# One product's two matmuls put into two different places of TensorE's order in a Mamba-2 mixer kernel

## The chip, the core and the metric

The kernel runs on one core of a Trainium2 chip. The metric is the device time of one execution in microseconds; shorter is better. In what follows PE is TensorE, the matrix engine (PEld its weight loads), DVE is VectorE, ACT is ScalarE, POOL is GpSimd and SP the engine that issues most DMAs. A line such as L846 is line 846 of the kernel.

## What is computed

A layer norm of x (4 sequences of 256 tokens, 512 channels) feeds two branches, a Mamba-2 state-space mixer and a gated feed-forward network. Their outputs are multiplied and added to x. Cut to what matters here, the mixer is:

```python
zxbcdt = hidden_states @ in_proj_w.T            # 512 -> 8192 gate, 8192 x, 1024 B, 1024 C, 128 dt
gate, xBC, dt = split(zxbcdt)
xBC = silu(causal_conv(xBC, conv_w, 4 taps) + conv_b)
x, B, C = split(xBC)                            # 128 heads of 64 channels, 8 groups
dt = softplus(dt + dt_bias)
# chunked scan: y = (C B^T * decay) (x * dt) + carried states
y = (Y_diag + Y_off) + D * x
y = y * silu(gate)
y = group_rms_norm(y) * norm_w
s = y @ out_proj_w.T
out = x_in + s * silu(ffn(layernorm(x_in)))
```

## The kernel before

A first stage (front, up to about 310 us of the span) makes the layer norm, the feed-forward branch, dt, and for each of the 8 groups the scores of B and C. Everything here concerns the second stage, a loop `for i in range(CT + 2)` over 64 channel tiles of 128 channels (two heads each). Iteration i works on three tiles at once: it projects tile i (`here`), computes the scan of tile i - 1 (`old`) and gates tile i - 2 (`older`). From iteration 10 on it also does a part of the output projection of an earlier group (`project_out`, with `og` the group and `on` the place 0 to 7 in it). The order on every engine is the order in which the code is written out by hand; each engine works off its own queue in that order and waits by semaphores for the others.

The projection of tile i takes seven products instead of eight, in Strassen's manner in the variant with fewer sums: a 2 x 2 arrangement of half the tokens by half of the 512 input channels, for gate and x together. A product is two logical matmuls of 128 x 128 weights by 512 tokens (k = 0 and 1); the profile shows each as two instructions, so a product is x4 there. They share three PSUM banks, px, pq and pz. In the order in which PE runs them, with the names that the text uses:

- P1: `product(px, a11, x11, True)`, L821. ACT then copies px to pz (L822), so that pz can go on by itself.
- P5: `product(pq, s1, t1, True)`, L830.
- P6: `product(px, s2, t2, False)`, L831, on top of P1 in px. ACT copies px out to gT (L832).
- P2: `product(pz, a12, x21, False)`, L837, on top of the copy in pz. Its sum is read much later, by the SiLU at L895.
- P7: `product(px, s3, t3, False)`, L845, again on px, after L832 has read it. ACT copies px out to xpad (L846).
- P4: `product(px, a22, t4, False)`, L876, once more on px, after L846 has read it. ACT copies it out at L877.
- P3: `product(pq, s4, x22, False)`, L881, on pq, after DVE has added the earlier sum in pq to xpad (L869, which itself follows L846). DVE adds P3's result to gT at L885.

All the products' matmuls stand under L173, the line in the helper `product`. In the profile's groups P1 is px<-xnT,w, P5 is pq<-xc,s, P6 is px<-xc,s, P2 is pz<-xnT,w, P7 and P4 are both px<-xc,w, and P3 is pq<-xnT,s.

Between them lies the work on tile i - 1. ACT finishes its convolution with a SiLU (`conv_silu`, L186: at the end of the iteration before for tiles from 9 on, at L825 of this one for tiles 0 to 8, as `LEAD` is 9) and makes exponentials of the decay (L615). DVE multiplies decays by scores (`meet`, L618 and L619). ACT starts the output banks (`y_begin`, L651). PE transposes block 0 of the tile, four transposes into the bank tp (T0, L624, called by `values_0`), and DVE scales it twice into v (L632). After P3, `values_1` does the same with block 1 (T1, and L641) in the same bank, of which there is one. In the end `y_products` (L665) multiplies v by the decays; DVE's convolution taps (L181), the sums of the next weights (L142 to L146) and a scan (L612) close the iteration. L672 (`y_gate`) opens the next one on DVE.

When `on` is 0 (iterations 10, 18, 26 and so on to 58) PE also runs `norm_sums` (L683, 16 small instructions) directly behind P7. When `on` is even, DVE makes `left_sums` (L701 to L704) ahead of L869.

So before the change PE's order around the place is P6, P2, P7, (norm_sums), T0, P4, P3, T1.

Of the kernel before, what the change touches and what calls it, by code (L numbers as in the profile page):

```python
# [57 lines left out]
KT = HID // P  # L58
# [23 lines left out]
def mixer_ffn(ctx: ExitStack, tc: tile.TileContext, x, in_w, conv_w, conv_b, dt_bias, a_log, d_col,  # L82
# [66 lines left out]
    def factors(w, s):  # L149
        a11, a12, a21, a22 = blocks(w)  # L150
        return a11, a12, a22, s[:, 0], s[:, 1], s[:, 2], a21

    def combine_w(w):
        s = scp.tile([P, 3, KT // 2, P], F32, name="s")
        for _ in combine_to(s[:, 0], s[:, 1], s[:, 2], blocks(w)[2], w):
            pass
        return factors(w, s)

    x11, x12, x21, x22 = [xnT[:, k:k + 2, h:h + HALF] for k in (0, 2) for h in (0, HALF)]
# [7 lines left out]
    def by_batch(v):  # L167
        return v.rearrange("p (b l) -> p b l", l=L)

    def product(pp, a, b, start):  # L170

        for k in range(KT // 2):
            nc.tensor.matmul(pp, a[:, k, :], b[:, k, :], start=start and k == 0,  # L173
                             stop=k == KT // 2 - 1, skip_group_check=not start)

# [13 lines left out]
    def front(pre, one_of, fp, f2, hp, wq):  # L189
# [223 lines left out]
        def bc_pieces(g):  # L413
# [7 lines left out]
            for a, b, to in ((a11, x11, cpad_h[0]), (s2, t2, cpad_h[1]), (s3, t3, bpad_h[1]),  # L421
                             (a22, t4, bpad_h[0])):
                product(px, a, b, a is a11)
                nc.scalar.copy(to, by_batch(px))
                if a is s2:
                    s = scp.tile([P, 3, KT // 2, P], F32, name="s")
                    held["a"] = factors(w, s)
                    sums = combine_to(s[:, 0], s[:, 1], s[:, 2], blocks(w)[2], w)
                if a is not a11:
                    next(sums, None)  # L430
                yield
            pz = ps_proj.tile([P, HALF], F32, name="pz", tag="proj")
            product(pz, a12, x21, True)
            nc.vector.tensor_add(cpad_h[0], cpad_h[0], by_batch(pz))
            pq = ps_proj.tile([P, HALF], F32, name="pq", tag="proj")
            product(pq, s1, t1, True)
            nc.vector.tensor_add(bpad_h[1], bpad_h[1], by_batch(pq))
            yield
# [136 lines left out]
    with (tc.manual_schedule(), tc.tile_pool(name="pre", bufs=NT) as pre,  # L575
# [3 lines left out]
        a = front(pre, one_of, fp, f2, hp, wq)  # L579
# [31 lines left out]
    def decay_scan(m):  # L611
        nc.vector.tensor_tensor_scan(m, m, after, 0.0, ALU.add, ALU.mult)  # L612

    def decay_exp(m):
        nc.scalar.activation(m, m, AF.Exp)  # L615

    def meet(m, off):
        nc.vector.tensor_mul(m, m, gm[:, 0:T])  # L618
        nc.vector.tensor_mul(off, off, gm[:, T:])  # L619

    def transposed(xT, c):
        tp = ps_t.tile([P, NB, P], F32, name="tp", tag="t")
        for b in range(NB):
            nc.tensor.transpose(tp[:, b, :], xT[:, b, c * P:(c + 1) * P], ident)  # L624
        return tp

    def values_0(ct, xT):

        tp, vs = transposed(xT, 0), []
        for f in (dt[:, 0], dt_tail):  # L630
            v = xsp.tile([P, NB, 2, HD], F32, name="v")
            nc.vector.tensor_tensor(  # L632
                v, tp.rearrange("p b (h d) -> p b h d", d=HD),
                f[:, :, 2 * ct:2 * ct + 2].unsqueeze(3).to_broadcast([P, NB, 2, HD]), ALU.mult)
            vs.append(v)
        return vs
# [9 lines left out]
    def y_begin(ct, xT):  # L646

        ps = []
        for i in range(2):
            py = ps_y.tile([P, 2, L], F32, name="py", tag="y")  # L650
            nc.scalar.mul(py, xT[:, 2 * i:2 * i + 2, :], dcol[:, ct:ct + 1])  # L651
            ps.append(py)
        return ps
# [107 lines left out]
    with tc.manual_schedule():  # L761
        nc.sync.dma_start(gm, scores[0])
        ms, offs = {0: load_rows(0)}, {0: load_off(0)}
        xTs, gTs, yps, wos, rights, toms = {}, {}, {}, {}, {}, {}
        sqacc = rs = ya = outs = left = nxt = ob = sa = sb = sc = None
        for i in range(CT + 2):
# [49 lines left out]
            if here:  # L816
                a11, a12, a22, s1, s2, s4, s3 = a
                px, pq, pz = [ps_proj.tile([P, HALF], F32, name=f"p{n}", tag="proj")
                              for n in "xqz"]
# [9 lines left out]
            if here:  # L829
                product(pq, s1, t1, True)  # L830
                product(px, s2, t2, False)  # L831
                nc.scalar.copy(gT[:, HALF:], px)  # L832
                if lead:
                    decay_exp(ms[i - 1][1])
                if i:
                    decay_scan(ms[i][0])
                product(pz, a12, x21, False)  # L837
            if old:
                meet(ms[i - 1][0], offs[i - 1][0])
                meet(ms[i - 1][1], offs[i - 1][1])  # L840
                if r == 0 and here:
                    nc.sync.dma_start(gm, scores[g])
                yps[i - 1] = y_begin(i - 1, xTs[i - 1])
            if here:
                product(px, s3, t3, False)  # L845
                nc.scalar.copy(xpad_h[1], by_batch(px))  # L846
            if og >= 0 and on == 0:
                sd = norm_sums(sqacc)
# [19 lines left out]
            if here:  # L868
                nc.vector.tensor_add(xpad_h[1], xpad_h[1], by_batch(pq))  # L869
            if old:  # L870
                vs = values_0(i - 1, xTs[i - 1])
            for n, turn in ((wg, PER_G - 1), (og, 0), (og, 1)):
                if i < CT + 1 and n >= 0 and on == turn:
                    toms[n].pop(0)()
# [32 lines left out]
            if here:  # L907
# [4 lines left out]
                if i + 1 <= EARLY:  # L912
                    s = scp.tile([P, 3, KT // 2, P], F32, name="s")
                    nc.sync.dma_start(s, early[i, :, 0:3])
                    a = factors(w, s)
                elif i + 1 < CT:
                    a = combine_w(w)
# [20 lines left out]
            if wg >= 0 and wg < G:  # L938
                if wn == 0:
                    wos[wg] = wop.tile([P, PER_G, HID], F32, name="wo")  # L940
                for k in range(PER_G):
                    if wn == come(k):
                        ct = wg * PER_G + k
# [14 lines left out]
        for b in range(NB):  # L958
            a, f, xb = whole[b]
# [75 lines left out]
```

## Time and profile before

| what | value |
|---|---|
| median of 3 runs | 1793.18 us (1792.14 to 1793.36) |
| the profiled execution, its own time | 1795.49 us |
| its span, from the first instruction to the last | 1793.0 us |
| PE busy | 1742.7 us (97%) |
| DVE busy | 1448.6 us (81%) |
| ACT busy | 1066.0 us (59%) |
| mean granted PE clock | 0.994 of full speed |

A profile is one execution. Its page gives the busy time of each engine, the chain of work that ended last, and groups of equal instructions with the idle time of the engine just ahead of them and what ended it. Matmuls are pipelined: one of 512 columns is shown with about 0.59 us although the next starts 0.43 us later, so a busy PE isn't PE at its peak, and an idle time is counted only from the modelled end of the last matmul.

### The profile page before, as it was taken

How to read it: one execution, taken by the hardware profiler on the slowest of the kernel's cores; microseconds unless marked ns; L12 is line 12 of the kernel's file. 1: busy time of each engine (PE TensorE's matmuls, PEld its weight loads, DVE VectorE, ACT ScalarE, POOL GpSimd, SP SyncE). 2: the span in 40 equal slices, each digit the busy share in tenths (PEclk: the TensorE clock that was granted, in tenths of full speed). 3: DMA queues.
4: the chain of work that ended last, by engine and by line, in shares of the span. 5: the costliest groups of instructions: out<-in, count | busy, mean ns of one | idle time of the engine just before them, and what ended most of it. 6: DMA issues, size and time to landing. Idle time of an engine off the chain costs nothing.

```text
span 1793.0 us, 22592 instructions
## 1 busy us (share of the span) xinstructions
PE 1742.7 (97%) x8494; PEld 1117.4 (62%) x8494; DVE 1448.6 (81%) x1740; ACT 1066.0 (59%) x1417; POOL 197.3 (11%) x239
## 2 busy tenths in 40 slices
PE   9999999999899999999999999999999999999989
PEld 6566666455466666666666666666666666666667
DVE  5758675799988888888888888888888888888846
ACT  4544343577666666666666666666666666666630
POOL 3221221000000000111011101110111011101110
PEclk9999999999999999999999999999999999999989
DMA  6254643566846665767676767676777676766674
GB/s 223 80 185 155 212 162 123 196 223 215 253 138 203 195 210 178 201 197 210 180 202 197 210 182 203 197 208 185 203 197 209 185 203 197 208 185 203 179 211 141
DMA packets 164235, 342.69 MB, mean 191 GB/s; under 512 B 15392, under 2 KB 55968, under 8 KB 164128
## 3 DMA queue, kind: packets, MB, share of 16 engines
q1 hardware_dynamic: 141296, 287.78, 46.3%
q0 software_dynamic: 22832, 53.49, 16.8%
q8 instruction: 67, 1.10, 0.2%
q14 instruction: 40, 0.33, 0.1%
HBM read 236.08 MB, written 76.28 MB: 174 GB/s over the span
## 4 chain that ended last, share of the span: by engine, by line
PE 89%; DVE 6%; ACT 4%; issue 1%; DMA 1%; ACTq 0%; DVEq 0%; SPq 0%
PE px L173 27%; PE po L721 21%; PE pq L173 13%; PE py L665 9%; PE pz L173 7%; PE pp L285 4%; PE pf L293 2%; ACT xpad L846 2%; PE tp L624 2%; PE pg L460 1%; DVE cT L181 1%; PE pv L683 1%; DVE xT L181 1%; DVE bT L181 1%; DVE m L612 0%
## 5 line engine op out<-in xcount | busy, mean ns | idle before, releaser
L173 PE MATMUL px<-xc,w 128*128 128x512 f32 x576 | 278.7, 606 | 19.4 <-ACT xpad L846 14.1
L612 DVE TENSOR_TENSOR_SCAN m<-m,after 128x1024 f32<-128x1024 f32 x128 | 292.0, 2282 | 0.0
L181 DVE SCALAR_TENSOR_TENSOR xT<-xpad,cw,xT 128x1024 f32<-128x1024 f32 x192 | 246.2, 1282 | 4.6
L173 PEld LDWEIGHTS px<-xc,w 128*128 128x128 f32 x576 | 104.2, 190 | 136.3 <-issue 97.4
L721 PE MATMUL po<-wo,ya 128*128 128x256 f32 x768 | 178.4, 382 | 0.0
L665 PE MATMUL py<-m,v 128*64 128x128 f32 x2048 | 162.2, 278 | 3.9 <-DVE v L641 3.9
L618 DVE TENSOR_TENSOR m<-m,gm 128x1024 f32<-128x1024 f32 x128 | 154.8, 1209 | 8.9 <-ACT m L615 8.9
L721 PEld LDWEIGHTS po<-wo,ya 128*128 128x128 f32 x768 | 142.6, 192 | 17.6 <-issue 0.3
L904 POOL DMA_DIRECT2D sqacc<-sq x55 | 46.9, 853 | 931.1 <-ACT sq L860 927.3
L173 PE MATMUL px<-xc,s 128*128 128x512 f32 x288 | 137.5, 600 | 5.0 <-ACT pz L822 2.2
L173 PE MATMUL px<-xnT,w 128*128 128x512 f32 x288 | 141.9, 615 | 0.0
L173 PE MATMUL pq<-xnT,s 128*128 128x512 f32 x288 | 136.2, 595 | 1.1 <-DVE xpad L869 1.1
L615 ACT ACTIVATE m<-m 128x1024 f32<-128x1024 f32 x128 | 135.4, 1058 | 0.7
L173 PE MATMUL pq<-xc,s 128*128 128x512 f32 x288 | 135.4, 592 | 0.3 <-DVE gT L885 0.3
L173 PE MATMUL pz<-xnT,w 128*128 128x512 f32 x288 | 135.3, 592 | 0.0
L665 PEld LDWEIGHTS py<-m,v 128*64 128x64 f32 x2048 | 118.0, 138 | 26.2 <-issue 19.7
L721 PE MATMUL po<-tw,sy 128*128 128x256 f32 x512 | 117.1, 382 | 1.2 <-ACT sa L775 1.2
L869 DVE TENSOR_TENSOR xpad<-xpad,pq 128x512 f32<-128x512 f32 x64 | 43.7, 683 | 80.3 <-ACT xpad L846 80.3
L721 PEld LDWEIGHTS po<-tw,sy 128*128 128x128 f32 x512 | 98.1, 192 | 15.2 <-ACT sa L775 1.6
L624 PEld LDWEIGHTS tp<-ident,xT 128*128 128x128 f32 x512 | 64.3, 143 | 67.8 <-issue 67.2
L672 DVE TENSOR_TENSOR yg<-py,gT 128x512 f32<-128x512 f32 x128 | 83.8, 678 | 22.7 <-PE py L665 22.7
L173 PEld LDWEIGHTS px<-xc,s 128*128 128x128 f32 x288 | 54.7, 192 | 73.0 <-issue 65.8
(172 smaller groups left out, 3059.8 us busy)
## 6 DMA issues: line engine op xcount, KB each, us to landing
m<-rows SPq DMA_DIRECT2D x128, 512.0 KB, 6.4
w<-in_in_w SPq DMA_DIRECT2D x133, 256.0 KB, 6.8
mo<-rows SPq DMA_DIRECT2D x128, 256.0 KB, 7.2
gated<-yg SPq DMA_DIRECT2D x64, 512.0 KB, 8.2
ya<-gated SPq DMA_DIRECT2D x30, 1024.0 KB, 7.1
sqacc<-sq POOLq DMA_DIRECT2D x55, 512.0 KB, 5.4
wo<-in_out_w SPq DMA_DIRECT2D x64, 256.0 KB, 7.1
acc<-sa POOLq DMA_DIRECT2D x24, 512.0 KB, 5.9
```

What stands on the lines that cost most here:

```text
L173: nc.tensor.matmul(pp, a[:, k, :], b[:, k, :], start=start and k == 0, stop=k == KT // 2 - 1, skip_group_check=not start)
L181: nc.vector.scalar_tensor_tensor(xT, xpad[:, :, k:k + L], cw[:, i, k:k + 1], xT, ALU.mult, ALU.add)
L285: nc.tensor.matmul(pp, w[:, k * P:(k + 1) * P], part[:, k, :], start=(k == 0 and part is xh), stop=(k == KT - 1 and part is xl))
L612: nc.vector.tensor_tensor_scan(m, m, after, 0.0, ALU.add, ALU.mult)
L615: nc.scalar.activation(m, m, AF.Exp)
L618: nc.vector.tensor_mul(m, m, gm[:, 0:T])
L624: nc.tensor.transpose(tp[:, b, :], xT[:, b, c * P:(c + 1) * P], ident)
L665: nc.tensor.matmul(py[d, q * P:(q + 1) * P], v[:, b, h, :], m, start=False, stop=stop, skip_group_check=True)
L672: nc.vector.tensor_mul(yg[:, 2 * i:2 * i + 2, :], ps[i], by_batch(gT[:, i * HALF:(i + 1) * HALF]))
L721: nc.tensor.matmul(po, a[:, k, :], b[:, k, :], start=start and k == 0, stop=k == HG - 1, skip_group_check=not start)
L869: nc.vector.tensor_add(xpad_h[1], xpad_h[1], by_batch(pq))
L904: nc.gpsimd.dma_start(sqacc, sq, accum_op=ALU.add)
```

## The change

P2's two matmuls are separated. The one for k = 0 stays where P2 was, between P6 and P7. The four transposes T0 are moved from `values_0` to directly behind it, still ahead of P7. The one for k = 1 moves behind P7 (and ahead of norm_sums, where there is one), so ahead of P4. `values_0` is handed the bank tp instead of filling it; DVE's two multiplications in it stay at their place. PE's order becomes P6, P2 (k = 0), T0, P7, P2 (k = 1), (norm_sums), P4, P3, T1. The other engines' orders and all DMAs are as before. In iteration 0 there is no T0, and in iteration 64 there are no products.

```diff
-    def product(pp, a, b, start):
+    def product(pp, a, b, start, ks=range(KT // 2)):
 
-        for k in range(KT // 2):
+        for k in ks:
             nc.tensor.matmul(pp, a[:, k, :], b[:, k, :], start=start and k == 0,
                              stop=k == KT // 2 - 1, skip_group_check=not start)
...
-    def values_0(ct, xT):
+    def values_0(ct, tp):
 
-        tp, vs = transposed(xT, 0), []
+        vs = []
         for f in (dt[:, 0], dt_tail):
...
-                product(pz, a12, x21, False)
+
+                product(pz, a12, x21, False, (0,))
             if old:
+                tp0 = transposed(xTs[i - 1], 0)
                 meet(ms[i - 1][0], offs[i - 1][0])
                 meet(ms[i - 1][1], offs[i - 1][1])
...
             if here:
                 product(px, s3, t3, False)
+                product(pz, a12, x21, False, (1,))
                 nc.scalar.copy(xpad_h[1], by_batch(px))
...
             if old:
-                vs = values_0(i - 1, xTs[i - 1])
+                vs = values_0(i - 1, tp0)
```

## The prediction

> **What bounds the kernel now.** I read the page first: shares of the engines, the chain that ended last, then the groups of instructions for the idle time ahead of TensorE.
>
> ```profile
> PE 1742.7 (97%) x8494; PEld 1117.4 (62%) x8494; DVE 1448.6 (81%) x1740; ACT 1066.0 (59%) x1417; POOL 197.3 (11%) x239
> PE 89%; DVE 6%; ACT 4%; issue 1%; DMA 1%; ACTq 0%; DVEq 0%; SPq 0%
> L173 PE MATMUL px<-xc,w 128*128 128x512 f32 x576 | 278.7, 606 | 19.4 <-ACT xpad L846 14.1
> ```
>
> TensorE (PE) is busy 97% of the span and makes 89% of the chain, so time is won only where PE stands still. The last line says where: ahead of the products px<-xc,w (P7 and P4), most of it ended by ACT's copy at L846. The view of waits, for PE alone, counts them:
>
> ```profile
> PE px L173 <- ACT xpad L846: 14.1, 57, 0.7
> PE px L173 <- ACT gT L832: 2.4, 1, 2.4
> ```
>
> Fifty-seven of the 64 iterations have that wait. P4 accumulates on the bank px that L846 has just read, so it waits for the copy. The chain of waits shows one such place (iteration 41) and the next iteration, which has none:
>
> ```profile
> 1192.85 1.72 PE px L173 x4
> 1194.56 1.72 PE pz L173 x4
> 1196.28 1.73 PE px L173 x4
> 1198.01 0.02 issue
> 1198.03 0.59 ACT xpad L846
> 1198.63 0.04 issue
> 1198.67 1.98 PE px L173 x4
> 1200.65 1.72 PE pq L173 x4
> ...
> 1217.83 1.72 PE px L173 x4
> 1219.54 1.68 PE pv L683 x16
> 1221.22 0.49 PE tp L624 x4
> 1221.71 1.72 PE px L173 x4
> ```
>
> The rows are P6, P2, P7, the wait, P4, P3; then P7, norm_sums, transposes, P4. In a stream a product takes 1.72 (four instructions, 0.43 apart) and four transposes 0.44. After the wait P4 takes 1.98: it also fills the pipeline, and its first weight load is no longer hidden. The wait therefore costs more than the idle column's 0.24: from P7's end to P4's end 0.65 + 1.98 = 2.63 us, where transposes and P4 in a stream need 0.44 + 1.72 = 2.16. So 0.47 us a time. Where norm_sums (1.68) stands in the hole, nothing is lost.
>
> The timeline of iteration 41 shows both copies and the gated weight load:
>
> ```profile
> 1194.60 0.59 ACT L832 COPY gT<-px 128x512 f32<-128x512 f32 x1 [1.89 <-PE px L173]
> 1198.03 0.59 ACT L846 COPY xpad<-px 128x512 f32<-128x512 f32 x1 [1.65 <-PE px L173]
> 1198.67 0.30 PEld L173 LDWEIGHTS px<-xc,w 128*128 128x128 f32 x2 [0.48 <-ACT xpad L846]
> ```
>
> Both copies find ACT idle (1.89 and 1.65 us), so each begins the moment PE ends. Each needs a cover of about 0.65 us on PE. Behind P6 the cover is P2, 1.72 us: 1.07 too much. Behind P7 it is the transposes, 0.44: 0.21 too little.
>
> **The change part by part.** It adds no instruction. It moves, on PE's queue alone, two matmuls of P2 (with two weight loads) past P7, and four transposes T0 ahead of P7 (past norm_sums too, where it stands). ACT, DVE, SP and POOL keep their order; no DMA moves.
>
> Part 1, T0 earlier. T0 needs xT of the iteration before and the bank tp free; behind it would wait P7 and all of PE. xT: the SiLU (L186) ended at 1208.40 + 1.14 = 1209.54 for an iteration whose P7 started at 1217.66. In iterations 1 to 9 the SiLU is younger (399.47 + 1.15 = 400.62 against a T0 at about 403.1), but stands on ACT ahead of the copy that P7 waits for in any case. tp: its last reader (L641) is 13 us old (1203.01). So T0 waits for nothing: cost 0. Were the SiLU late, all of PE would be held. T0 next to a 512-column product has no price of its own: T1 sits between P3 and the next product now, and the chain gives 0.44 for it.
>
> Part 2, cover behind P6: half of P2 (0.86) and T0 (0.44) = 1.30 us. The copy needs 0.65, so 0.65 is spare: cost 0. In iteration 0 there is no T0 and the cover is 0.86, still enough but for the weight load. In iterations 1 to 9 this copy comes later, as ACT has a SiLU, two table loads and an exponential ahead of it; its end (402.90 + 0.56 = 403.46 in iteration 5), 1.7 us after P6's last matmul began, leaves P7 about 0.1 late.
>
> Part 3, cover behind P7: half of P2, 0.86, for 0.65. PE's stream is whole again, with a small remainder. A weight load normally starts when the matmul before it starts, 0.43 ahead; P4's first one carries the wait and is let go only about 0.02 before its matmul is due. After the old wait the second matmul followed the load by 0.54 instead of 0.43, so an isolated load costs 0.11, of which about 0.05 (0.65 + 1.98 against 0.86 + 1.72 = 2.58) remains. Here the Trainium skill speaks against the change ("TensorE: Matmul & The Clock Gate", Part 3, The mechanism): a weight load overlaps running matmuls only if its row group differs. All loads here use all 128 rows. By that rule no cover would hide P4's load, 0.19 us would be paid, and the gain would be 0.47 - 0.19 = 0.28 an iteration, 13 us in 47. The trace does not bear it out: 0.19 us loads lie under 512-column matmuls which still follow each other at 0.43. I take the trace.
>
> Sum per iteration, from P6's end to P4's end: before 1.72 + 1.72 + 0.65 + 1.98 = 6.07 (the rows: 1194.56 to 1200.65 = 6.09); after 0.86 + 0.44 + 1.72 + 2.63 = 5.65. Gain 0.43. Its bounds: 0.47 if the load hides wholly; 0.34 if 0.19 - 0.05 shows.
>
> **Which iterations keep it.** Of the 57 waits, 47 lie in iterations 11 to 63. The other six there (18, 26, ... 58) hold norm_sums: no wait before, nothing won. Next in line in the 47 is L869 on DVE, which P3 waits for. In odd iterations it starts behind L846 and moves with it. In even ones DVE has left_sums first:
>
> ```profile
> 1266.27 0.30 PEld L173 LDWEIGHTS px<-xc,w 128*128 128x128 f32 x2 [0.48 <-ACT xpad L846]
> 1266.78 0.68 DVE L869 TENSOR_TENSOR xpad<-xpad,pq 128x512 f32<-128x512 f32 x1
> ```
>
> It ends at 1267.46; with 0.05 for the signal P3's load may go at 1267.51. P3's first matmul, now at 1268.10, would be due at 1267.67: 0.16 later, more than the 0.11 of an isolated load. It just fits, so even iterations keep 0.43 too; the lower bound for these 20 is half. DVE as a whole has room: in the 180.5 us from 1215.5 (eight iterations) it is busy 155.0. Further on, PE waits for nothing in that stretch except L846 (1.7 us, 7 times), and all that feeds later steps (L885, T1, the taps) follows P3.
>
> Iterations 2 to 9 keep nothing, since P3 waits there for L869 at the end of an unbroken DVE chain:
>
> ```profile
> 407.74 0.68 DVE L869 TENSOR_TENSOR xpad<-xpad,pq 128x512 f32<-128x512 f32 x1
> 408.48 0.30 PEld L173 LDWEIGHTS pq<-xnT,s 128*128 128x128 f32 x2 [0.83 <-DVE xpad L869]
> ```
>
> P4 can come sooner there, P3 not. They also absorb the 0.1 of part 2. Iteration 10 holds norm_sums. Iteration 1: PE waits 2.4 for L832, 0.4 more without that half of P2, and P7 after it is slow already (3.68 for 1.88); half of P2 then covers L846; I put 0 (at worst 0.4). Iteration 0: P7 ends about 0.7 earlier (cover 0.86 for 1.72), DVE stood 7.25 idle ahead of L869, and the chain over the taps into iteration 1 carries that: 0.7.
>
> Sum: 47 x 0.43 + 0.7 = 20.9 us. The profiled execution took 1795.49 us around a span of 1793.0; the runs' median is 1793.18, 2.3 below. The difference is applied to the median: 1772.3 us.
>
> **The rivals.** (a) DVE takes over in even iterations: L869 and left_sums hold P3, and the wait moves from P4 to P3. For it: 0.16 of room only. Against it: L869 follows PE's last y_products at a fixed distance. Then 27 x 0.43 + 20 x 0.2 + 0.7 = 16, and with the load exposed in all 27 x 0.34 + 20 x 0.17 + 0.7 = 13: 1777 to 1780. Chance 0.12.
> (b) Slower: P7 comes to wait for L832. Its cover falls from 1.72 to 1.30 against 0.65. It decides once the copy is more than 0.65 late, and outweighs the gain beyond about 1.0 (1.0 - 0.65 + 0.11 for the bare load = 0.46). One exponential (1.06) slipping in ahead of it would cost P7 0.41 + 0.11 = 0.52, net 0.09 x 47 = 4 us slower: 1797; two would cost 1.58, net 1.15 x 47 = 54: 1847. Against it: ACT idles 1.89 us before that copy and its order is unchanged. Chance 0.05, with any unseen wait at T0 in it.
> (c) The change does nothing: P4's wait was really for something else (a weight, another bank), or PE's time is given back at y_products. For it: a wait for several semaphores shows only the last. Against: P4 starts 0.04 after the copy's end every time, and PE has no other repeated wait behind it. 1793. Chance 0.04.
>
> **How the numbers follow.** Likeliest case 0.79: 1772.3, its own range 1769 to 1777 (47 x 0.47 + 0.7 = 22.8 down to 47 x 0.34 + 0.7 = 16.7, and one us of scatter). The range reaches to rival (a): 1768.5 to 1779.5. A difference under 0.2%, 3.6 us, can't be told from none here. Faster 0.91 (likeliest and a), same 0.04 (c), slower 0.05 (b).
>
> **What would show it.** Right: PE's wait on L846 falls from 14.1 us to a few; the chain runs P6, P2 half, T0, P7, P2 half, P4, with steps of 0.86, 0.44 and 1.72; the distance between iterations shrinks by 0.43 from iteration 11 on, and not at all from 2 to 9 or over norm_sums; L846's copy starts 0.43 earlier behind P6. Wrong: idle PE ahead of P7 ended by L832 (b), ahead of P3 ended by L869 in even iterations (a), ahead of tp ended by ACT or DVE (part 1), or the same distances as before (c).

## The result, and the profile after

| kernel | median | runs | ratio to before, 95% interval |
|---|---|---|---|
| before | 1793.24 us | 1792.14 to 1793.36 | |
| the change | 1775.07 us | 1773.71 to 1775.34 | 0.9899 [0.9881, 0.9916] |

The change is faster by 18.2 us, 1.0%. The forecast was 1772.3, with a range from 1768.5 to 1779.5. The profiled execution of the changed kernel took 1773.71 us around a span of 1771.7. In the new code L846 has become L849, L869 has become L872, L877 is L880 and L885 is L888; L832 and L624 keep their numbers.

Of the page, the lines that answer to the three shown of before:

```profile
PE 1733.2 (98%) x8494; PEld 1110.2 (63%) x8494; DVE 1447.3 (82%) x1740; ACT 1065.8 (60%) x1417; POOL 198.2 (11%) x239
PE 85%; DVE 11%; ACT 2%; issue 2%; DMA 1%; ACTq 0%; DVEq 0%; SPq 0%
L173 PE MATMUL px<-xc,w 128*128 128x512 f32 x576 | 279.2, 607 | 4.9 <-ACT xpad L424 2.7
```

The number of instructions on every engine is as before. What has gone is most of the idle time ahead of P7 and P4: 4.9 us for 19.4, and what is left of it belongs mainly to the first stage (L424). DVE's share of the chain has grown from 6% to 11% because the chain now runs over DVE in iterations 2 to 9, though these take as long as before. The view of waits for PE no longer has a row for the copy behind P7; these are its rows on the second stage that matter here:

```profile
PE py L665 <- DVE v L641: 4.1, 10, 0.4
PE pq L173 <- DVE xpad L872: 3.3, 8, 1.4
...
PE px L173 <- ACT gT L832: 2.2, 1, 2.2
```

L872 (L869 before) holds P3 in eight places, against one before. They are iterations 2 to 9, in which P4 now ends sooner and P3 stands waiting for DVE. The wait for L832 is iteration 1's, as before. In iterations 2 to 9 P7 comes 0.10 to 0.15 us late behind that copy (the prediction said about 0.1), which costs nothing as P3 waits for DVE there; from iteration 11 on P7 is never late.

The chain of waits, at an even iteration (22):

```profile
760.28 0.86 PE pz L173 x2
761.14 0.44 PE tp L624 x4
761.58 1.72 PE px L173 x4
763.30 0.86 PE pz L173 x2
764.15 1.80 PE px L173 x4
765.96 1.72 PE pq L173 x4
```

These are half of P2, T0, P7, the other half, P4, P3. No step of ACT is left in it. P4 takes 1.80 and not 1.72: that is the remainder of the late weight load. The timeline (an odd iteration) shows where it comes from:

```profile
1185.47 0.59 ACT L849 COPY xpad<-px 128x512 f32<-128x512 f32 x1 [1.22 <-PE px L173]
1185.70 0.59 PE L173 MATMUL pz<-xnT,w 128*128 128x512 f32 x1
...
1186.11 0.30 PEld L173 LDWEIGHTS px<-xc,w 128*128 128x128 f32 x2 [0.65 <-ACT xpad L849]
1186.13 1.97 PE L173 MATMUL px<-xc,w 128*128 128x512 f32 x4
...
1187.93 1.88 PE L173 MATMUL pq<-xnT,s 128*128 128x512 f32 x4
```

P4's matmul is due at 1185.70 + 0.43 = 1186.13 and starts then by the record, but its weight load was let go only at 1186.11, by the end of the copy (1186.06) and 0.05 for the signal. So the array is not yet loaded, and the four instructions take 1.97, against 1.88 of a group of four in a stream, as P3 in the last row.

From the start of P6's last matmul in iteration 11 to the same place in iteration 63 the trace of before gives 1172.8 us, that of the change 1153.9: 18.9 us in these 52 iterations. This distance is used below, since it leaves out the first stage, the early iterations and the end.

### The profile page after: what moved, and what is told of

It reads as the page before. It is cut to its first block, busy times and chain, and to the rows that moved or that the text cites. A ratio compares the mean times of both kernels' runs of the same rounds, so it can differ in the third digit from the quotient of the medians.

```text
span 1771.7 us, 22592 instructions
## 1 busy us (share of the span) xinstructions
PE 1733.2 (98%) x8494; PEld 1110.2 (63%) x8494; DVE 1447.3 (82%) x1740; ACT 1065.8 (60%) x1417; POOL 198.2 (11%) x239
## 4 chain that ended last, share of the span: by engine, by line
PE 85%; DVE 11%; ACT 2%; issue 2%; DMA 1%; ACTq 0%; DVEq 0%; SPq 0%
PE px L173 24%; PE po L721 22%; PE pq L173 13%; PE py L665 9%; PE pz L173 6%; PE pp L285 4%; PE tp L624 3%; DVE m L612 2%; PE pf L293 2%; DVE xT L181 2%; PE pg L460 1%; DVE cT L181 1%; PE pv L683 1%; DVE m L618 1%; DVE mo L619 1%
## 5 line engine op out<-in xcount | busy, mean ns | idle before, releaser
L173 PEld LDWEIGHTS px<-xc,w 128*128 128x128 f32 x576 | 99.3, 190 | 115.4 <-issue 69.4
L173 PE MATMUL pz<-xnT,w 128*128 128x512 f32 x288 | 145.8, 592 | 0.0
L665 PEld LDWEIGHTS py<-m,v 128*64 128x64 f32 x2048 | 117.8, 137 | 26.2 <-issue 19.6
L624 PEld LDWEIGHTS tp<-ident,xT 128*128 128x128 f32 x512 | 63.8, 141 | 71.9 <-issue 57.6
L832 ACT COPY gT<-px 128x512 f32<-128x512 f32 x64 | 37.4, 584 | 105.1 <-PE px L173 105.1
```

The lines of the kernel that those rows point to most:

```text
L665: nc.tensor.matmul(py[d, q * P:(q + 1) * P], v[:, b, h, :], m, start=False, stop=stop, skip_group_check=True)
```

## The experiments

The theory: each of the two copies out of px needs a certain amount of other PE work behind the product that it reads; before the change the place behind P6 had far more than it needs and the place behind P7 too little, and the change does nothing but share it out. The edits are shown against the changed kernel. The main rival: T0's earlier place is what helps, because DVE then finds tp ready. The second: the way from P7 over ACT to P4 isn't what holds P4.

### P2 split, T0 left behind P7

```diff
             if old:
-                tp0 = transposed(xTs[i - 1], 0)
                 meet(ms[i - 1][0], offs[i - 1][0])
...
             if old:
+                tp0 = transposed(xTs[i - 1], 0)
                 vs = values_0(i - 1, tp0)
```

> P2 is split, but T0 stays behind P7: the order is P6, half of P2, P7, half of P2, T0, P4. Theory (each ACT copy needs a cover of about 0.65 us of PE work, wherever the cover comes from): behind P6 0.86, behind P7 0.86 + 0.44, so both copies are hidden; the small remainder of a late weight load (0.09) moves from P4 to P7. Time as with the whole change, 1774 to 1777. Rival (T0's earlier place does the work, because DVE finds tp ready sooner): at most half of the gain is left, 1783 or more.

Measured: 1774.73 us, ratio 0.9893 [0.9878, 0.9908], the same as the whole change. Its chain of waits:

```profile
760.05 0.86 PE pz L173 x2
760.91 1.80 PE px L173 x4
762.71 0.86 PE pz L173 x2
763.57 0.44 PE tp L624 x4
764.01 1.72 PE px L173 x4
```

The 1.80 has moved from P4 to P7, which now has the cover of 0.86; P4 with 0.86 + 0.44 takes 1.72. From iteration 11 to 63 it needs 1154.0 us, for 1153.9. So moving T0 is not needed, and the rival falls: T0 only decides which of the two products pays the remainder.

### T0 moved, P2 left whole

```diff
-                product(pz, a12, x21, False, (0,))
+                product(pz, a12, x21, False)
...
                 product(px, s3, t3, False)
-                product(pz, a12, x21, False, (1,))
```

> T0 is moved ahead of P7, P2 stays whole: the order is P6, P2, T0, P7, P4. Theory: the hole behind P7 has no cover at all, so P4 waits from P7's end 0.65 and restarts with 1.98; from P6's end to P4's end 1.72 + 0.44 + 1.72 + 2.63 = 6.51 against 6.07 before, 0.44 x 47 = 21 us slower, with a little from iterations 2 to 9: 1812 to 1818. Rival (T0 earlier is what helps): faster than before, under 1793.

Measured: 1816.29 us, ratio 1.0125 [1.0108, 1.0142]. The wait that the change took away grows here instead:

```profile
PE px L173 <- ACT xpad L848: 38.5, 57, 0.7
```

and in the chain of waits nothing stands between P7 and the copy's end:

```profile
772.82 1.73 PE px L173 x4
774.55 0.02 issue
774.57 0.60 ACT xpad L848
775.17 0.04 issue
775.21 1.98 PE px L173 x4
```

Each of the 57 waits is longer by (38.5 - 14.1) / 57 = 0.43 us, which is T0's 0.44. Half of the change alone thus costs 22 us, where both halves win 18: T0 earlier is of no use by itself and does harm without P2's half in its place.

### T0 behind P6, the whole of P2 behind P7

```diff
-                product(pz, a12, x21, False, (0,))
...
                 product(px, s3, t3, False)
-                product(pz, a12, x21, False, (1,))
+                product(pz, a12, x21, False)
```

> T0 alone stands behind P6 and the whole of P2 behind P7: the order is P6, T0, P7, P2, P4. Theory: the wait moves from P4 to P7 at the same price, 0.65 + 1.98 for P7 and then P2 and P4 in a stream: 2.63 + 1.72 + 1.72 = 6.07 as before. The six iterations with norm_sums now pay 0.45 each, and iterations 2 to 9 some 0.2 each: 1795 to 1800. PE's wait ahead of P7, ended by the copy into gT, appears about 55 times with 0.2 to 0.25 us each. Rival (only P4's wait costs, P7 is not held by its copy): as fast as the change, 1775 or below.

Measured: 1798.4 us, ratio 1.0026 [1.0016, 1.0036]. The two covers have changed places, and so has the wait:

```profile
PE px L173 <- ACT gT L832: 21.8, 64, 2.2
```

```profile
742.56 1.73 PE px L173 x4
744.29 0.02 issue
744.32 0.59 ACT gT L832
744.91 0.04 issue
744.95 1.98 PE px L173 x4
```

It is the picture of before with P7 in P4's place and L832 in L846's: the same 0.65 from a product's end to the next one's start, the same 1.98 behind it. In the iterations with the wait both ways nothing changes; the loss of 4.5 us is what was expected of the norm_sums iterations, which cover P7 only, and of the early ones. From iteration 11 to 63 it is 1176.1 - 1172.8 = 3.3 us, six times 0.55.

### T0 in two halves

```diff
-    def transposed(xT, c):
-        tp = ps_t.tile([P, NB, P], F32, name="tp", tag="t")
-        for b in range(NB):
+    def transposed(xT, c, bs=range(NB), tp=None):
+        if tp is None:
+            tp = ps_t.tile([P, NB, P], F32, name="tp", tag="t")
+        for b in bs:
...
+            if old:
+                tp0 = transposed(xTs[i - 1], 0, (0, 1))
+            if here:
                 product(pz, a12, x21, False, (0,))
             if old:
-                tp0 = transposed(xTs[i - 1], 0)
...
                 product(px, s3, t3, False)
-                product(pz, a12, x21, False, (1,))
                 nc.scalar.copy(xpad_h[1], by_batch(px))
+            if old:
+                transposed(xTs[i - 1], 0, (2, 3), tp0)
             if og >= 0 and on == 0:
                 sd = norm_sums(sqacc)
+            if here:
+                product(pz, a12, x21, False, (1,))
```

> Two of the four transposes ahead of P2's first half and two ahead of its second (which stands behind norm_sums where there is one): P6, 2 transposes, half of P2, P7, 2 transposes, half of P2, P4. Cover 1.08 us behind each of P6 and P7, and the last instruction ahead of the gated weight load is a long matmul. Theory: the last 0.09 us of the load at P4 is hidden too, less 0.02 to 0.05 in even iterations where P3 now waits for DVE's L869: 47 x 0.07 + 6 x 0.05 = 3.5 us under the change, 1770 to 1773. Rival (a full-height weight load never hides under a running matmul, as one reading of the skill has it; or DVE holds P3): no gain over the change, 1774 to 1776.

Measured: 1769.87 us, ratio 0.9866 [0.9851, 0.9880]. The chain of waits at iteration 22:

```profile
758.11 0.22 PE tp L625 x2
758.33 0.86 PE pz L173 x2
759.19 1.72 PE px L173 x4
760.91 0.22 PE tp L625 x2
761.13 0.86 PE pz L173 x2
761.99 1.72 PE px L173 x4
763.70 1.75 PE pq L173 x4
```

Both P7 and P4 now take 1.72: the full-height weight load lies wholly under the long matmul ahead of it. The timeline of P4 shows it:

```profile
761.58 0.43 PEld L173 LDWEIGHTS px<-xc,w 128*128 128x128 f32 x2 [0.42 <-ACT xpad L850]
761.82 1.02 PE L173 MATMUL px<-xc,w 128*128 128x512 f32 x2
...
763.46 0.30 PEld L173 LDWEIGHTS pq<-xnT,s 128*128 128x128 f32 x2 [0.59 <-DVE xpad L877]
```

The first load (0.19 us) is let go 0.24 us ahead of its matmul, against 0.02 in the change. What comes next is there to be seen too, in the last row: P3, 1.75, is held by DVE in this even iteration, by 0.03 us (L877 here is L869 of the kernel before). This version beats the kernel before and the change.

### The copy behind P6 made twice

If the change lives on cover that had lain unused behind P6, then the changed kernel must feel a longer copy there, and the kernel before must not.

```diff
                 nc.scalar.copy(gT[:, HALF:], px)
+                nc.scalar.copy(gT[:, HALF:], px)
```

In the changed kernel:

> The changed kernel, with ACT's copy of px into gT behind P6 made twice (0.59 us more before P7 may start). Theory: the change has spent the spare cover behind P6. P7 may go 1.86 us after P6's last matmul began and is due at 1.73, with 0.11 for its bare load it loses 0.24: 53 iterations (norm_sums included) x 0.24 = 13, and 1 to 2 us in iterations 0 to 9: 1787 to 1792. Rival (P7 is not held by this copy, or DVE and ACT have the say over the iteration's length): no more than 2 us, under 1777; or the whole 0.59 x 64 = 38 us, over 1800, if nothing at all was spare.

Measured: 1790.22 us, ratio to before 0.9977 [0.9969, 0.9984]: 3.8 us under the kernel before beside it (1793.99), where the change had won 18.2. The timeline shows P7 let go by the second copy:

```profile
741.71 0.59 ACT L832 COPY gT<-px 128x512 f32<-128x512 f32 x1 [1.89 <-PE px L173]
742.33 0.58 ACT L833 COPY gT<-px 128x512 f32<-128x512 f32 x1
742.96 0.30 PEld L173 LDWEIGHTS px<-xc,w 128*128 128x128 f32 x2 [0.24 <-ACT gT L833]
742.96 1.98 PE L173 MATMUL px<-xc,w 128*128 128x512 f32 x4
```

In the kernel before, with the same edit:

> The kernel before, with the same copy made twice. Theory: P7 is due at 2.15 there, the doubled copy lets it go at 1.86, 0.29 ahead and more than the 0.11 of a bare load: nothing in iterations 11 to 63, 1 to 2 us in iterations 0 to 9: 1793 to 1797, a ratio to before of 1.000 to 1.002. Rival (the extra work on ACT itself costs): as much slower here as with the change, 1800 or more.

Measured: 1795.63 us, ratio 1.0009 [1.0002, 1.0016]. From iteration 11 to 63 it takes 1172.8 us, to 0.01 us the same as without the second copy, so what little was lost was lost elsewhere. The same 0.6 us of work on ACT is thus free in one kernel and costs 1167.5 - 1153.9 = 13.6 us of loop in the other. The change has turned spare cover into speed, and too little of it is left for a second copy.

### The change and the halves once more

The medians gave the change 18 us and the traces 20, so both kernels ran again on one chip.

> The changed kernel itself once more, beside the kernel before on the same chip, for a narrower ratio. The traces put the loop's gain at 20 us, the medians at 18. Theory (only scatter lies between them): 19 to 21 us, a ratio of 0.9883 to 0.9894. Rival (one to three us are given back behind the loop, where the trace of one execution doesn't show it): 17 to 18.5 us, 0.9897 to 0.9905.

Measured: 1772.3 us against 1792.36, 20.1 us, ratio 0.9888 [0.9873, 0.9902]. The interval holds both theories' numbers; its middle is the first one's, and the first runs' interval holds it too. Nor do the traces show a loss behind the loop: from the start of P6's last matmul in iteration 63 to the end of the span they have 102.3 us before, and 100.9 and 101.1 in the two profiles of the change.

> The version with T0 in two halves once more, on the same chip as the change, to put the two side by side. Theory (the last 0.09 us of the weight load is hidden, 0.06 to 0.09 an iteration): 3 to 5 us under the change. Rival (the gap of 5 us in the first runs was scatter between chips): within 1.5 us of it.

Measured: 1769.77 us, ratio 0.9868 [0.9851, 0.9884], 2.5 us under the change, for 5.2 in the first runs: between what the two theories had said. The loop decides: from iteration 11 to 63 the halves take 1150.6 and 1150.5 us in two profiles, the change 1153.9 and 1153.8. The gain is 3.3 us in these iterations.

## Why the prediction was right, step by step

**The price of the wait.** The prediction said that a wait costs 0.47 us and not the 0.24 of the idle column, since the restart takes 1.98 for 1.72. The reason held and the size was a little low: by the starts of the matmuls (table below) a wait cost 0.50. An iteration became shorter by 0.42 us (21.548 to 21.130 in odd iterations, 23.274 to 22.857 in even ones), far more than 0.24.

**The cover.** In iterations 11 to 63 of all kernels with a single copy, the second matmul behind a copy of 0.59 us starts not sooner than 1.80 us after the start of the last matmul ahead of that copy. In iteration 41 of before these are 0.59 until that matmul is shown as ended, 0.04 to the copy, 0.59 for the copy, 0.05 until the weight load is let go, and 0.53 from there to the second matmul. Without a wait the second matmul would start 0.43 + cover + 0.43 after it. The runs, with PE's work in between (medians over the 47 iterations without norm_sums; within a row they differ by less than 0.01):

| cover | seen behind | second matmul | without a wait | lost |
|---|---|---|---|---|
| 0 | P7, T0 moved alone | 1.80 | 0.86 | 0.94 |
| 0.44 | P7, before | 1.80 | 1.30 | 0.50 |
| 0.86 | P7, the change | 1.80 | 1.72 | 0.09 (1.803 less 1.716) |
| 1.08 | P7, T0 in halves | 1.94 | 1.94 | 0 |
| 1.30 | P7, P2 split alone | 2.16 | 2.16 | 0 |

So 0.94 us (1.80 less 0.86) would hide a copy wholly; the runs bear it out with 0.86, which was short by 0.09, and 1.08, which was enough. The prediction took 0.65 for the copy. As a measure of the cover that leaves out the 0.16 by which a matmul is shown as running on when the next could already start (0.59 less 0.43), and the 0.10 that a bare weight load adds (0.53 less 0.43).

Two terms of the sum were therefore mis-sized, both by some 0.03 to 0.04: the wait, 0.50 for 0.47, and the remainder of the load, 0.09 for 0.05. They cancel, so the close agreement of the gain is in part luck: 0.418 measured, 0.42 by the prediction's own steps (6.07 less 5.65), where its sum took 0.43. The rule weighed there (the Trainium skill, "TensorE: Matmul & The Clock Gate", Part 3, The mechanism), that a weight load overlaps running matmuls only if its row group differs, would have left the cover of 1.08 with a visible load. It left none.

**Which iterations.** Iterations 11 to 63 without norm_sums kept it all, odd and even alike, as said: 47 x 0.418 = 19.6 us. Rival (a), DVE holding P3 in even ones, did not come: P3's 0.16 of room was enough, and with T0 in halves, where P3 is due 0.08 sooner, it was just not (0.03). Iterations 2 to 9 kept nothing (17.27 us each, before and after), and iteration 0 gave its 0.7. What was not foreseen is small: in the six norm_sums iterations P4 now follows those small instructions at once, and its second matmul starts 0.05 later than before (6.52 us for 6.47 behind P6's last; with T0 in halves 6.52 too). Why a product starts up worse behind norm_sums than behind T0 was not tried; in iteration 1 P4 came about 0.1 sooner.

**The sum.** 20.9 us predicted, 20.2 in the loop by the traces (the start of P6's last matmul in iteration 63 moved from 1690.71 to 1670.78, which is 19.9; 0.4 for P4 behind it, less 0.2 by which the loop began sooner), 18.2 by the first medians and 20.1 by the second. The prediction's 1772.3 stood 2.8 under the first median. That the second median is 1772.3 to the digit is chance: the kernel before stood at 1792.36 there, 0.8 under the 1793.18 that the forecast was reckoned from.

**The rest.** (b), a wait at P7, appears where cover is taken from P6: in nine early iterations with P2 split alone, at every P7 with T0 alone there, and with the copy made twice. So it was a real danger, and its margin was smaller than said: 0.36 us (1.30 less 0.94) and not 0.65. With the copy made twice P7's second matmul starts 2.42 us after P6's last and not 1.80; 0.62 more would have been within the margin of 0.65, but P7 lost 0.26 (2.42 less 2.16). (c) fell with the first trace.

## What to carry to other kernels

Where an accumulator bank is read between two products, ask at each such place how much other work of the same engine stands in it, and share that work out so that every place has just enough: here about 0.94 us of TensorE work for a 0.59 us copy. A long filler can be divided where its instructions don't have to follow each other at once; here the two matmuls of one accumulation stood apart, with a product into another bank between them, and took 0.86 + 0.86 for 1.72. Then count what the donor has left, because the next longer copy will find it spent.

## What the runs showed of the hardware

The granted clock goes with a part of the scatter between executions. Of the 35 executions of the kernel before that ran beside those with the copy made twice, seven had a mean clock of 0.994 and a median of 1794.8 us, and six had 0.996 and 1792.8 us. In iteration 10 PE stands idle for 2.2 us ahead of P6 in every kernel. In five of the ten profiles the four matmuls behind it then run at half the clock, in the other five at the full one. The timelines of the kernel before and of the one with T0 alone moved, and the windows over the same matmuls with the granted clock (the column 0.51 or 1.00 behind POOL):

```profile
490.35 3.68 PE L173 MATMUL px<-xc,s 128*128 128x512 f32 x4 [2.22 <-ACT pz L822]
```

```profile
490.30:493.70 3.40, 3.35 (x4) 1.51 (x5) 3.40 (x4) 0.98 (x1) 0.00 (x0) 0.51 1.02 346
```

```profile
492.79 1.98 PE L173 MATMUL px<-xc,s 128*128 128x512 f32 x4 [2.22 <-ACT pz L822]
```

```profile
492.70:494.70 2.00, 1.91 (x5) 0.95 (x6) 2.00 (x2) 1.02 (x2) 0.00 (x0) 1.00 0.94 358
```

The same pause of 2.22 us is followed by 3.68 us in one and 1.98 in the other, 1.7 us apart. The code alone doesn't decide it: the kernel with T0 in halves took 1.98 there in one of its profiles and 3.59 in the other. Iteration 1, with a pause of 2.2 to 2.4 us, does the same: slow in the profiles of before (3.68) and of the change (3.56), at full speed in the second profile of the change (1.98). Two such places make some 3 us that have nothing to do with the edit. What decides it was not tried.
